# Two attention layers on one core: layer 1's regrouping transfers handed out one at a time, its next loads in 128 KB pieces, small transfers on GpSimd's queue

## The chip, the cores and the metric

The kernel runs on one core of a Trainium2 chip. Its time is the device time of one execution in microseconds (us). A core has a matrix engine (TensorE, PE in the profile, with its weight loads shown apart as PEld), VectorE (DVE), ScalarE (ACT), GpSimd (POOL) and SyncE (SP). SP computes nothing here: it issues DMA transfers, in the order in which they are written, and stops at a transfer whose semaphores have not come yet. All transfers run on the core's 16 DMA engines.

## The reference

```
x = x + layer0(groupnorm(x))     # 8 images, 512 channels, 32*32 = 1024 tokens
x = x + layer1(groupnorm(x))
```

Layer 0 is an attention with 8 heads after another group norm. Layer 1, which the change concerns, is an attention that mixes its heads before the softmax and normalises after it:

```
q, k, v = w_q x, w_k x, w_v x              # 8 heads of 64
attn = (q.k) * scale                       # per head, 1024 x 1024
attn = einsum('gh,bhqT->bgqT', w_head, attn)
attn = softmax(attn);  attn = (attn - mean) / sqrt(var + eps) * gamma + beta
out  = w_proj (attn . v) + b_proj
```

Everything is float32.

## The kernel before

**Stages.** Layer 0 runs first, image by image, and leaves its result in DRAM (`x1_d`). Layer 1 then takes the eight images in turn (`for b in range(B)`, from about 2000 us of the profile on). One image is an attention stage of 37 half-steps and a stage of projections (keys and values of the next image, output of this one, queries of the next one), in which TensorE is filled by large products.

**A half-step.** `Attention1.half_step(x, ag)` does six groups of products on TensorE, for several stages of the pipeline at once: `scores(x, 0)`, `mix(y, 0)`, `values(w, 0)`, `scores(x, 1)`, `mix(y, 1)`, `values(w, 1)`, with `y = x - 4` (`MLAG`) and `w = x - 5`. `x` counts 32 half-steps (`NX`) and then some that only drain the pipeline. `scores` makes q.k for two heads; VectorE or ScalarE copies the result into a tile `raw[t]`, `t = x // 2`. When `x` is odd the tile is complete: 128 partitions by 16 KB. To mix heads, heads must lie along the partitions, so the tile is rearranged by DMA: `regroup(t)` issues eight transfers of 256 KB (`R_ORDER`), each from every eighth partition of `raw[t]` to a tile `re[t, r]`. `mix` multiplies these by the small matrix `wmix` (32 products in the source for each of its two calls, 64x64 blocks; two of its calls use the same eight tiles), and ScalarE takes the exponential. In the next half-step `squares`, `sum_e`, `sum_e2` and `values` use it.

**Order.** The order of instructions on every engine is the order in which the code is written; an `Agenda` (`ag.at(x, f)`) puts a function at the end of a given half-step. Buffers set the rest: `raw` has two buffers, so the first copy of tile t+2, in half-step 2t+4, must wait until all eight transfers of tile t have landed; `re` has sixteen, so the transfers of tile t reuse tiles that `mix` reads up to the second call of half-step 2t+1. Scores, mix, totals and projections share three PSUM buffers (`m_psum`).

**SP's queue before the change.** In an odd half-step the eight regrouping transfers are issued together, between `scores(x, 1)` and `mix(y, 1)` in the program's order. In the same queue, from the agenda, are: the next image's input (`load_y`, four transfers of 512 KB after half-steps 6, 8, 10, 12) and its key and value weights (`load_w`, 256 KB each, after half-steps 14 to 28), and, three times in an image before the last time, the small transfers of the softmax's sums. For the latter, `totals(qb)` sums by products and copies a row, and two transfers `c<-row` spread it over partitions; two half-steps later `reciprocals(qb)` takes 1/x and writes it to DRAM (`zd<-rz`), and two transfers read it back to all partitions (`rzb<-zd`, 256 KB each); `divide(qb)` multiplies with it, after half-step x+5.

Of the kernel before, what the change touches and what calls it, by code (L numbers as in the profile page):

```python
# [9 lines left out]
F32 = mybir.dt.float32  # L10
# [8 lines left out]
P = 128  # L19
# [448 lines left out]
def tile_two_attention_layers(  # L468
# [527 lines left out]
    with ExitStack() as l1:  # L996
# [27 lines left out]

        y_t, qo_t, k_t, v_t, w_t = {}, {}, {}, {}, {}

        def load_w(key, src, chunks=range(NCC)):
            tag = {"v": "wtB", "p": "wp"}.get(key[0], "wtA")
            for c in chunks:
                if c == 0:  # L1030
                    w_t[key] = wtpool.tile(
                        [P, NCC, C], F32, tag=tag, name=f"w{key[0]}_{key[1]}"
                    )
                nc.sync.dma_start(out=w_t[key][:, c], in_=src[ts(c, P)])
# [230 lines left out]
        class Attention1:  # L1265
            def __init__(self, b):
                self.b = b
                self.raw, self.re, self.e, self.e2 = {}, {}, {}, {}

            def scores(self, x, i):  # L1270

                b, t, hp = self.b, x // 2, x % 2 * 2 + i
                qb, kb = t // NKB, t % NKB
                nm = f"s1_{b}_{x}_{i}"
                ps = m_psum(nm)
                pv = ps.rearrange("p m (j k) -> p m j k", j=2)
                for j in range(2):
                    for c in range(2):
                        for m in range(2):
                            r = slice(m * D, m * D + D)  # L1280
                            nc.tensor.matmul(  # L1281
                                pv[c * D : c * D + D, m, j],
                                qo_t[b][r, 2 * qb + j, hp, ts(c, D)],
                                k_t[b][r, hp, ts(kb, KB)], start=True, stop=True,
                            )
                if x % 2 == 0 and i == 0:
                    self.raw[t] = rawpool.tile([P, H, 2, KB], F32, tag="raw", name=f"raw_{b}_{t}")
                dst = self.raw[t][:, 2 * hp : 2 * hp + 2]
                if i == 0 and (x < MLAG or x % 2):
                    nc.vector.tensor_copy(dst, pv)  # L1290
                else:
                    nc.scalar.copy(dst, pv)  # L1292

            def regroup(self, t):

                raw = self.raw.pop(t)
                for r in R_ORDER:
# [3 lines left out]
                    nc.sync.dma_start(out=self.re[t, r], in_=raw[r::NR])  # L1301

            def mix(self, y, j):

                t, kc = y // 2, y % 2
                if j == 0:
                    self.e[y] = epool.tile([P, 2, T], F32, tag="e", name=f"e1_{self.b}_{y}")
                ps = m_psum(f"m1_{self.b}_{y}_{j}")
                for r in R_ORDER:
                    for c in range(2):  # L1310
                        k0 = kc * P + c * D
                        for a in range(2):
                            rows = slice(a * D, a * D + D)
                            nc.tensor.matmul(  # L1314
                                ps[c * D : c * D + D, a, ts(r, D)],
                                self.re[t, r][rows, j, k0 : k0 + D],
                                wmix[rows].rearrange("p g i -> p (g i)"),
                                start=True, stop=True,
                            )
                nc.scalar.activation(self.e[y][:, j], ps.rearrange("p a c -> p (a c)"), AF.Exp)  # L1320

            def squares(self, y, j):
                if y % QLAG == 0:
# [23 lines left out]
            def values(self, y, w):  # L1347

                b, t, kc = self.b, y // 2, y % 2
                kc = t % NKB * 2 + kc  # L1350
                if kc == 0 and w == 0:
                    self.acc = [
                        ps_a.tile([P, 2, QB], F32, tag=f"a{i}", name=f"a1_{b}_{y}_{i}")
                        for i in range(2)
                    ]
                e = self.by_head(self.e[y].rearrange("p j c -> p (j c)"))
                for g in range(4 * w, 4 * w + 4):
                    s, two = g // 2 % 2, g % 2
                    nc.tensor.matmul(  # L1359
                        self.acc[w][two * D : two * D + D, s].rearrange(  # L1360
                            "p (c i) -> p c i", i=Q8
                        ),
                        v_t[b][:, kc, ts(g, D)], e[:, g],
                        start=(kc == 0 and s == 0), stop=(kc == NT - 1),
                        skip_group_check=True,
                    )

            def leave(self, qb):

# [12 lines left out]
            def totals(self, qb):  # L1382


                ps = m_psum(f"t_{self.b}_{qb}")
                row = e2pool.tile([P, 2, FB], F32, tag="e2", name=f"row_{self.b}_{qb}")
                for m, z in ((1, self.z2), (0, self.z)):
                    for c in range(4):
                        nc.tensor.matmul(  # L1389
                            ps[c * 32 : c * 32 + 32, m].rearrange(  # L1390
                                "p (g c i) -> p g c i", g=4, i=Q8
                            ),
                            ones[:, :32],
                            self.by_head(z[:, c // 2])[:, c % 2 * 4 : c % 2 * 4 + 4],
                            start=True, stop=True, tile_position=(0, c * 32),
                        )
                nc.vector.tensor_copy(row[:, 1], ps[:, 1])
                nc.scalar.copy(row[:, 0], ps[:, 0])
                self.rows = []
                for m in range(2):  # L1400
                    c = stat.tile([P, 16], F32, tag=f"c{m}", name=f"c{m}_{self.b}_{qb}")
                    nc.sync.dma_start(out=c, in_=row[0::32, m])
                    self.rows.append(c)

            def reciprocals(self, qb):

                b = self.b
                zc, z2c = self.rows
                rz = stat.tile([P, 16], F32, tag="rz", name=f"rz1_{b}_{qb}")
                nc.vector.reciprocal(rz, zc)  # L1410
                zd = dram.tile([2, T], F32, tag=f"zd_{b}_{qb}", name=f"zd_{b}_{qb}")
                nc.sync.dma_start(out=zd, in_=rz)
                self.rzb = zpool.tile([P, T], F32, tag="rzb", name=f"rzb_{b}_{qb}")
                for two in range(2):
                    nc.sync.dma_start(
                        out=self.rzb[two * D : two * D + D], in_=zd[two].partition_broadcast(D)
                    )
# [55 lines left out]
            def half_step(self, x, ag):  # L1473
# [21 lines left out]
                    self.values(w, 0)  # L1495
                if x < NX:
                    self.scores(x, 1)
                    if x % 2:
                        self.regroup(x // 2)
                if 0 <= y < NX:  # L1500
                    self.mix(y, 1)
                if 0 <= w < NX:
                    self.values(w, 1)
                    self.e.pop(w)
                    if w % QLAG == QLAG - 1:
                        qb = w // QLAG
                        self.totals(qb)
                        if qb < NQB - 1:
                            ag.at(x + 2, lambda: self.reciprocals(qb))
                            ag.at(x + 5, lambda: self.divide(qb))  # L1510
                ag.run(x)


# [16 lines left out]
        for b in range(B):  # L1530
# [107 lines left out]
```

## Time and profile before

| what | value |
|---|---|
| median of 11 runs | 4574.57 us (4559.16 to 4720.16) |
| the profiled execution's own time | 4585.32 us |
| its span, first to last instruction | 4583.4 us |
| TensorE clock granted, mean | 0.995 |
| PE busy | 4383.5 us (96%) |
| DVE, ACT busy | 2475.5 us (54%), 2286.5 us (50%) |
| attention stage of one image, 2330 to 2512 us: PE, DVE, ACT busy | 167.76, 140.32, 147.65 of 182 us |
| the same stage: DMA share, bytes | 0.73 of 16 engines, 185 GB/s |
| regrouping transfers | 1024 of 256 KB, all from SP |

A line of a group of instructions reads: source line, engine, operation, what it writes and reads, shapes, how often; then busy time and the mean of one in ns; then the idle time of the engine just before them and what ended most of it. "issue" is idle time that ended with nothing that the profile can name. A wait is put down to the latest of the events that it waited for. The DMA share is the mean busy share of the 16 DMA engines.

### The profile page before, as it was taken

The page shows a single profiled execution, that of the slowest core. Times are in us where ns is not written, and L with a number is a line of the kernel's source. Part 1 is how long each engine was busy: PE and PEld are TensorE (multiplying, and loading weights), DVE is VectorE, ACT ScalarE, POOL GpSimd, SP SyncE. Part 2 cuts the span into 40 slices and gives each one's busy share as a digit, 9 for nine tenths or more (in the row PEclk, how much of TensorE's full clock was granted, in tenths as well). Part 3 has the DMA queues.
Part 4 walks back from the last instruction along what each step waited for, and adds up shares of the span by engine and source line. Part 5 has one row for each costly group of instructions (what it writes and reads, how often), then busy time and mean ns, then how long its engine had stood idle before and what let it go on. Part 6 is the DMA issues. An engine that isn't in the chain of part 4 may idle for free.

```text
span 4583.4 us, 129918 instructions
## 1 busy us (share of the span) xinstructions
PE 4383.5 (96%) x58560; PEld 2243.0 (49%) x58560; DVE 2475.5 (54%) x3396; ACT 2286.5 (50%) x2651; POOL 6.6 (0%) x14
## 2 busy tenths in 40 slices
PE   7999999999999999899999999999999999999998
PEld 3343434343434343356466466465466465465565
DVE  1727272727272727258367367376277276376376
ACT  1707070707070706058267277177177276276385
POOL 0000000000000000000000000000000000000000
PEclk9999999999999999999999999999999999999999
DMA  2010101010101000257267176275275375374464
GB/s 74 16 42 16 42 16 42 16 42 16 42 16 42 16 23 16 79 147 185 69 165 186 53 187 162 70 187 146 75 193 134 94 177 131 107 180 115 115 164 128
DMA packets 242885, 426.38 MB, mean 93 GB/s; under 512 B 63120, under 2 KB 63120, under 8 KB 242320
## 3 DMA queue, kind: packets, MB, share of 16 engines
q1 hardware_dynamic: 239744, 413.77, 33.7%
q8 instruction: 460, 7.54, 0.7%
q10 hardware_dynamic: 2304, 4.20, 0.3%
q14 instruction: 105, 0.86, 0.1%
q0 software_dynamic: 272, 0.02, 0.0%
HBM read 114.32 MB, written 34.08 MB: 32 GB/s over the span
## 4 chain that ended last, share of the span: by engine, by line
PE 92%; issue 3%; ACT 2%; DVE 2%; DMA 1%; SPq 1%; POOL 0%; DVEq 0%; POOLq 0%
PE a L1359 11%; PE s L1281 10%; PE m L1314 10%; PE a L876 9%; PE s L850 9%; PE pk L1081 5%; PE pk L797 5%; PE pv L1105 5%; PE pq L1137 5%; PE pq L797 5%; PE pv L820 5%; PE pp L797 5%; PE pp L1167 4%; PE t L1389 2%; PE z L898 1%
## 5 line engine op out<-in xcount | busy, mean ns | idle before, releaser
L1314 PE MATMUL m<-wmix,re 64*64 64x64 f32 x32768 | 612.1, 219 | 92.8 <-issue 86.0
L1314 PEld LDWEIGHTS m<-wmix,re 64*64 64x64 f32 x32768 | 593.5, 135 | 196.9 <-issue 134.0
L1320 ACT ACTIVATE e<-m 128x1024 f32<-128x1024 f32 x512 | 528.0, 1031 | 145.0 <-PE m L1314 141.7
L1359 PE MATMUL a<-e,v 128*64 128x256 f32 x4096 | 564.9, 393 | 33.2 <-ACT q L1380 20.9
L1337 DVE TENSOR_TENSOR z<-z,e 128x1024 f32<-128x1024 f32 x448 | 540.2, 1220 | 88.8 <-ACT e L1320 88.3
L1341 DVE TENSOR_TENSOR z<-z,e 128x1024 f32<-128x1024 f32 x448 | 535.6, 1220 | 75.4 <-ACT e L1330 75.0
L855 ACT ACTIVATE e<-s 128x1024 f32<-128x1024 f32 x512 | 498.4, 1026 | 147.9 <-PE s L850 147.9
L1281 PE MATMUL s<-k,q 64*64 64x256 f32 x8192 | 557.2, 389 | 6.0 <-issue 5.7
L850 PE MATMUL s<-q,k 64*64 64x512 f32 x4096 | 489.7, 591 | 3.0 <-ACT q L785 1.5
L863 DVE TENSOR_TENSOR zacc<-zacc,e 128x1024 f32<-128x1024 f32 x384 | 469.6, 1223 | 41.8 <-ACT e L855 15.3
L876 PE MATMUL a<-e,v 64*64 64x512 f32 x4096 | 484.1, 589 | 0.0
L1330 ACT ACTIVATE e<-e 128x1024 f32<-128x1024 f32 x448 | 461.7, 1061 | 0.0
L1292 ACT COPY raw<-s 128x1024 f32<-128x1024 f32 x368 | 373.1, 1016 | 165.7 <-PE s L1281 137.5
L1281 PEld LDWEIGHTS s<-k,q 64*64 64x64 f32 x8192 | 271.3, 133 | 270.7 <-issue 178.0
L1359 PEld LDWEIGHTS a<-e,v 128*64 128x64 f32 x4096 | 252.4, 136 | 156.8 <-issue 24.6
L876 PEld LDWEIGHTS a<-e,v 64*64 64x64 f32 x4096 | 156.6, 133 | 282.8 <-issue 282.8
L850 PEld LDWEIGHTS s<-q,k 64*64 64x64 f32 x4096 | 152.1, 133 | 286.8 <-issue 261.3
L1290 DVE COPY raw<-s 128x1024 f32<-128x1024 f32 x144 | 176.3, 1224 | 137.3 <-PE s L1281 116.2
L1081 PE MATMUL pk<-y,wk 128*128 128x512 f32 x512 | 230.3, 604 | 5.2 <-DVE y L1066 4.9
L797 PE MATMUL pp<-xa,wp 128*128 128x512 f32 x512 | 224.1, 598 | 5.9 <-DVE xa L938 5.9
L797 PE MATMUL pk<-n,w 128*128 128x512 f32 x512 | 225.5, 599 | 4.2 <-issue 4.2
L1105 PE MATMUL pv<-wv,y 128*128 128x512 f32 x512 | 225.5, 596 | 0.0
(190 smaller groups left out, 3276.0 us busy)
## 6 DMA issues: line engine op xcount, KB each, us to landing
re<-raw SPq DMA_DIRECT2D x1024, 256.0 KB
x<-in_x_dram SPq DMA_DIRECT2D x32, 512.0 KB
rzb<-zd SPq DMA_DIRECT2D x128, 128.0 KB
x<-x SPq DMA_DIRECT2D x32, 512.0 KB
y<-x SPq DMA_DIRECT2D x32, 512.0 KB
rzb<-zd SPq DMA_DIRECT2D x64, 256.0 KB
xs<-x SPq DMA_DIRECT2D x28, 512.0 KB
out_dram<-xs SPq DMA_DIRECT2D x28, 512.0 KB
```

The costliest lines, as they stand in the source:

```text
L797: nc.tensor.matmul(ps[:, f], w[:, c, o0 + oc * P : o0 + (oc + 1) * P], rhs[:, c, ts(f, FB)], start=(c == 0), stop=(c == NCC - 1),)
L850: nc.tensor.matmul(ps[c * D : c * D + D, m], k[r, hp, k0 : k0 + D], q[r, hp, ts(f, FB)], start=True, stop=True,)
L855: nc.scalar.activation(e[i], ps, AF.Exp)
L863: nc.vector.tensor_add(zacc[g], zacc[g], e[i])
L876: nc.tensor.matmul(acc[g][a][m * D : m * D + D], v[rows, kc, ts(2 * hp + m, D)], e[i][rows, m], start=(kc == 0), stop=(kc == NG - 1),)
L1281: nc.tensor.matmul(pv[c * D : c * D + D, m, j], qo_t[b][r, 2 * qb + j, hp, ts(c, D)], k_t[b][r, hp, ts(kb, KB)], start=True, stop=True,)
L1314: nc.tensor.matmul(ps[c * D : c * D + D, a, ts(r, D)], self.re[t, r][rows, j, k0 : k0 + D], wmix[rows].rearrange("p g i -> p (g i)"), star ...
L1320: nc.scalar.activation(self.e[y][:, j], ps.rearrange("p a c -> p (a c)"), AF.Exp)
L1330: nc.scalar.activation(e2, self.e[y][:, j], AF.Square)
L1337: nc.vector.tensor_add(self.z[:, j], self.z[:, j], self.e[y][:, j])
L1341: nc.vector.tensor_add(self.z2[:, j], self.z2[:, j], self.e2[j])
L1359: nc.tensor.matmul(self.acc[w][two * D : two * D + D, s].rearrange("p (c i) -> p c i", i=Q8), v_t[b][:, kc, ts(g, D)], e[:, g], start=(kc ...
```

## The change

In words:

- `regroup` no longer issues eight transfers together. After `scores(x, 1)` of an odd half-step (x of 5 to 31) the eight are put on a list (`self.due`), and one is taken from it after each of `mix(y, 0)`, `values(w, 0)`, `mix(y, 1)`, `values(w, 1)`. `behind(dma, ins)` adds a dependency: the transfer waits on SP until the last product of that group is done. Up to half-step 4, and from 32 on, what is on the list is issued at once, without this dependency.
- The next image's input and its key and value weights become pieces of 128 KB (`y_piece`: 32 partitions by 4 KB, 16 pieces; `w_piece`: 64 partitions by 2 KB, 8 pieces for each weight), on a list `self.pieces`; from half-step 5 on one is issued behind each `scores`. Before, they were 512 KB and 256 KB transfers from the agenda.
- `c<-row` and `zd<-rz` go to GpSimd's queue for the first three of an image's four blocks (`queue(qb)`). The two transfers `rzb<-zd` of these blocks are put at the head of the list of pieces one half-step after `reciprocals`. `divide` comes one half-step later.

The diff, cut to its core:

```diff
+        def behind(dma, ins):
+            tc.add_manual_dep(
+                dma.ins, ins.ins.name,
+                mybir.DependencyInfo(
+                    mybir.DependencyClass.Sync, mybir.DependencyReason.DATA
+                ),
+                reason="one at a time",
+            )
+        def w_piece(key, src, i):
...
+            c, r = i // 2, i % 2 * D
+            return nc.sync.dma_start(
+                out=w_t[key][r : r + D, c], in_=src[c * P + r : c * P + r + D]
+            )
+        def y_piece(b, i):
...
+            c, r = i // 4, i % 4 * 32
+            return nc.sync.dma_start(
+                out=y_t[b][r : r + 32, c], in_=x1_d[b][c * P + r : c * P + r + 32, :]
+            )
...
             def scores(self, x, i):
...
+                if x > MLAG:
+                    self.piece(last)
+                if x % 2 and i == 1:
+                    self.due = [(t, r) for r in R_ORDER]
...
-            def regroup(self, t):
-                raw = self.raw.pop(t)
-                for r in R_ORDER:
+            def regroup(self, ins=None, n=1):
+                for t, r in self.due[:n]:
                     self.re[t, r] = repool.tile(
                         [P, 2, KB], F32, tag="re", name=f"re_{self.b}_{t}_{r}"
                     )
-                    nc.sync.dma_start(out=self.re[t, r], in_=raw[r::NR])
+                    dma = nc.sync.dma_start(out=self.re[t, r], in_=self.raw[t][r::NR])
+                    if ins is not None:
+                        behind(dma, ins)
+                self.due = self.due[n:]
+            def piece(self, ins=None, n=1):
+                for fn in self.pieces[:n]:
+                    dma = fn()
+                    if ins is not None:
+                        behind(dma, ins)
+                self.pieces = self.pieces[n:]
...
             def mix(self, y, j):
...
+                self.regroup(last)
...
             def values(self, y, w):
...
+                self.regroup(last)
...
-                    nc.sync.dma_start(out=c, in_=row[0::32, m])
+                    self.queue(qb).dma_start(out=c, in_=row[0::32, m])
...
+            def queue(self, qb):
+                return nc.sync if qb == NQB - 1 else nc.gpsimd
-            def reciprocals(self, qb):
+            def reciprocals(self, qb, ag=None, x=None):
...
-                nc.sync.dma_start(out=zd, in_=rz)
+                self.queue(qb).dma_start(out=zd, in_=rz)
...
+                    ag.at(x + 1, lambda: self.pieces.__setitem__(slice(0, 0), spread))
...
                     self.scores(x, 1)
-                    if x % 2:
-                        self.regroup(x // 2)
                 if 0 <= y < NX:
                     self.mix(y, 1)
+                if x <= MLAG or x >= NX:
+                    self.regroup(n=NR)
+                if x >= NX:
+                    self.piece(n=len(self.pieces))
...
-                            ag.at(x + 2, lambda: self.reciprocals(qb))
-                            ag.at(x + 5, lambda: self.divide(qb))
+                            ag.at(x + 2, lambda: self.reciprocals(qb, ag, x + 2))
+                            ag.at(x + 6, lambda: self.divide(qb))
...
+                a.pieces += [lambda i=i: y_piece(b + 1, i) for i in range(4 * NCC)]
+                a.pieces += [lambda i=i: w_piece(("k", b + 1), wkT, i) for i in range(2 * NCC)]
+                a.pieces += [lambda i=i: w_piece(("v", b + 1), wvT, i) for i in range(2 * NCC)]
                 for c in range(NCC):
-                    ag.at(6 + 2 * c, lambda c=c: load_y(b + 1, [c]))
-                    ag.at(14 + 2 * c, lambda c=c: load_w(("k", b + 1), wkT, [c]))
-                    ag.at(22 + 2 * c, lambda c=c: load_w(("v", b + 1), wvT, [c]))
                     ag.at(24 + c, lambda c=c: normalize1(b + 1, [c]))
```

More of the change, by code (lines that the diff above doesn't have):

```diff
@@ L1025, in tile_two_attention_layers @@
         y_t, qo_t, k_t, v_t, w_t = {}, {}, {}, {}, {}
+        def behind(dma, ins):
+            tc.add_manual_dep(
+                dma.ins,
+                ins.ins.name,
+                mybir.DependencyInfo(
[4 more added lines that the diff above has]
+        def w_piece(key, src, i):
+            tag = {"v": "wtB", "p": "wp"}.get(key[0], "wtA")
+            if i == 0:
+                w_t[key] = wtpool.tile([P, NCC, C], F32, tag=tag, name=f"w{key[0]}_{key[1]}")
+            c, r = i // 2, i % 2 * D
[3 more added lines that the diff above has]
+        def y_piece(b, i):
+            if i == 0:
+                y_t[b] = ypool.tile([P, NCC, T], F32, tag="y", name=f"y_{b}")
+            c, r = i // 4, i % 4 * 32
+            return nc.sync.dma_start(
+                out=y_t[b][r : r + 32, c], in_=x1_d[b][c * P + r : c * P + r + 32, :]
+            )
         def load_w(key, src, chunks=range(NCC)):
@@ L1268, in __init__ @@
                 self.raw, self.re, self.e, self.e2 = {}, {}, {}, {}
+                self.due, self.pieces = [], []
             def scores(self, x, i):
@@ L1280, in scores @@
                             r = slice(m * D, m * D + D)
-                            nc.tensor.matmul(
+                            last = nc.tensor.matmul(
                                 pv[c * D : c * D + D, m, j],
@@ L1313, in mix @@
                             rows = slice(a * D, a * D + D)
-                            nc.tensor.matmul(
+                            last = nc.tensor.matmul(
                                 ps[c * D : c * D + D, a, ts(r, D)],
@@ L1358, in values @@
                     s, two = g // 2 % 2, g % 2
-                    nc.tensor.matmul(
+                    last = nc.tensor.matmul(
                         self.acc[w][two * D : two * D + D, s].rearrange(
@@ L1411, in reciprocals @@
                 zd = dram.tile([2, T], F32, tag=f"zd_{b}_{qb}", name=f"zd_{b}_{qb}")
-                nc.sync.dma_start(out=zd, in_=rz)
+                self.queue(qb).dma_start(out=zd, in_=rz)
                 self.rzb = zpool.tile([P, T], F32, tag="rzb", name=f"rzb_{b}_{qb}")
-                for two in range(2):
-                    nc.sync.dma_start(
-                        out=self.rzb[two * D : two * D + D], in_=zd[two].partition_broadcast(D)
-                    )
+                rzb = self.rzb
+                spread = [
+                    lambda two=two: nc.sync.dma_start(
+                        out=rzb[two * D : two * D + D], in_=zd[two].partition_broadcast(D)
+                    )
+                    for two in range(2)
+                ]
+                if ag is None:
+                    for fn in spread:
+                        fn()
+                else:
+                    ag.at(x + 1, lambda: self.pieces.__setitem__(slice(0, 0), spread))
                 col = B * H + NQB * b + qb
```

## The prediction

> **What bounds the kernel now.** I read the page first: PE is busy 4383.5 of 4583.4 us, and the chain that ended last is 92% PE and 3% "issue". So only TensorE's own pauses can be won, and I looked next at the groups of layer 1 and at who PE waited for from 2050 us on (columns: total us, times, longest).
>
> ```profile
> PE m L1314 <- issue: 80.5, 90, 2.7
> PE a L1359 <- ACT q L1380: 20.9, 24, 0.9
> PE a L1359 <- issue: 10.5, 14, 1.7
> PE t L1389 <- DVE z L1341: 6.1, 8, 0.9
> PE s L1281 <- issue: 5.3, 9, 1.2
> PE m L1314 <- DMA re<-raw: 4.6, 10, 0.9
> ```
>
> The reader should see that the data are hardly ever late (4.6 us for the regrouped tiles) and that 80.5 + 10.5 + 5.3 = 96 us end with nothing named. What is that? A pause in the middle of one `mix`, on the timeline of PE:
>
> ```profile
> 2748.08 0.75 PE L1314 MATMUL m<-wmix,re 64*64 64x64 f32 x39
> 2749.88 0.62 PE L1314 MATMUL m<-wmix,re 64*64 64x64 f32 x25 [1.04 <-issue]
> ```
>
> Its tiles had been used by the `mix` before it, so no transfer was missing. The DMA table has a kind of traffic that no line of the kernel issues:
>
> ```profile
> q1 hardware_dynamic: 239744, 413.77, 33.7%
> q8 instruction: 460, 7.54, 0.7%
> ```
>
> That is 460 packets of 16 KB: instructions. TensorE's two rows have 2 x 58,560 of them, 255 per packet. Laying the trace's packet records of q8 over PE's instructions, I find that 122 of layer 1's 159 PE pauses over 0.15 us (131.7 us in all) end between 1 and 2 us after the end of such a packet, and that most neighbouring pauses lie whole multiples of 256 instructions apart. These are late instruction fetches. What makes them late: of the fetches that began after 2.5 us in which the DMA engines were under 0.2 busy, 94 were followed by 0.013 us of pause in the mean; of those after more than 0.8 busy, 217 were followed by 0.44 us. SP's queue and the DMA share show where the full stretches come from:
>
> ```profile
> 2716.56 6.87 SPq L1301 DMA_DIRECT2D re<-raw  x8
> 2723.48 0.65 SPq L1034 DMA_DIRECT2D wk<-in_wkT_dram  x1
> 2730.87 6.60 SPq L1301 DMA_DIRECT2D re<-raw  x8
> ...
> 2716.50:2728.00 11.50, 11.14 (x338) 7.98 (x336) 9.99 (x16) 10.39 (x12) 0.00 (x0) 1.00 0.85 208
> 2753.90:2757.20 3.30, 3.10 (x88) 2.04 (x86) 3.30 (x4) 1.69 (x3) 0.00 (x0) 1.00 0.12 34
> ```
>
> The last two are stretches of time (PE, PEld, DVE, ACT, POOL busy, clock, DMA share, GB/s): a burst of eight, with one weight load, keeps the DMA engines 0.85 x 11.5 = 9.8 us busy; then they idle. So 256 KB costs 9.8/9 = 1.07 us of all engines; SP issues one in about 0.67 us (median), so two or three pile up.
>
> **What the Trainium skill says.** "Runtime: NRT & Kernel Launch", section "Instruction fetch mechanics": instructions come in blocks of 16 KiB (256 instructions) through a DMA queue of the sequencer's own, and the cost is "mostly hidden". The trace agrees on the block (7.54 MB / 460) and not on the hiding (96 us). "DMA: Bandwidth & Descriptors", "Queues, rings and completion order": a DMA engine alternates between queues by packet of some 9 to 17 descriptors, so a fetch waits at least for what is in service. A 256 KB transfer is eight 2 KB packets of the trace per engine, 1.07 us. On GpSimd's queue the same page ("Anatomy of one DMA") has about 2 us per transfer; this trace's eight small ones took 7.2 to 8.4 us, and I use those. "SBUF — State Buffer", "SBUF: two separate sides": GpSimd's descriptors can be held up by VectorE's fast copies; no run here shows it, and the copies in question take 0.69 us.
>
> **The change part by part.** Without pauses half of a half-step takes 2.97 us (scores start at 2716.59, 2719.56, 2722.53).
>
> 1. *Regrouping one by one.* Removed: the pile. Each 2.97 us two transfers are released, 2.14 us of DMA, plus a piece of 128 KB (half of 1.07: 0.53; a 512 KB input load shows 2.0 us): 2.67 us, a share of 0.90 where pieces run (38 in the 54 slots) and 0.72 elsewhere. The engines remain that full, but what a fetch finds ahead of it is one transfer, at most 1.07 us, rather than two or three. About 290 fetches fall in the attention stages; 96 us is 0.33 us each. Bounds: 0.013 us each (all relieved, saves 92 us) to 0.33 us (nothing). I take 0.125, about a quarter of the way from 0.013 to 0.44, since the share stays high and only the queue's depth falls: 36 us stay, **-60 us**.
>
> 2. *The last of the eight goes later.* Before, all eight were out about 7 us after the first; now the eighth waits for `values(w, 0)` of half-step 2t+3. From there to the copy that reuses `raw` lie scores 0.92 + mix 1.04 + values 1.01 + scores 0.92 = 3.89 us, and its products begin 0.91 us later (7/8 of a mix). An issue moves its first data 1.1 us after it starts (2712.43 to 2713.54 in the packet records); + 1.07 + some 0.3 to be seen (estimate) = 2.5 us. A piece ahead of it is served before (0.53 against 2.05 us of lead). Margin 1.4 us to the copy, 2.3 us to the products: 0 us. This is the step with least cover. If landing took 5 us or more, ScalarE, which has the copy in even half-steps and is busy 147.65 of 182 us, would stop 1.1 us for each of 112 tiles (14 of 16 per image x 8); its slack takes most of that.
>
> 3. *New waits on SP.* Each transfer waits for a product. Behind it in SP are only transfers whose products come later, in PE's own order; six issues per half-step at 0.55 to 0.67 us are 3.3 to 4.0 of 5.94 us: 0. The first of eight also waits for ScalarE's copy, as before (2716.54 end of copy, 2716.56 issue).
>
> 4. *Small transfers on GpSimd.* SP stood 433 us at `c<-row` (32 times, most of it at an image's end, which stays) and 107.6 us at `rzb<-zd`. Taking it away frees SP for about 3 us, 24 times; PE hardly waited on that, so 0 to -4 us. On GpSimd `c<-row` takes some 8 us after 2711.2, about 2720; `reciprocals` came at about 2723.9, at the faster pace 2723: hidden, margin 2 to 3 us; if late, VectorE stops, at most 2 us x 24, inside its slack (140.32 of 182). `zd<-rz` then lands near 2731.5, but the pieces `rzb<-zd` want issuing at the `scores` of x+4, near 2728.5: SP stops up to 3 us, as it did before (4.5 us at 2725). It delays the third and fourth of eight, which have over 5 us in hand: 0. `divide` one half-step later: nothing needs it before the output projection.
>
> 5. *Pieces.* Same bytes, 32 + 6 transfers where there were 12 + 6. They are done by half-step 24, when `normalize1` begins (32 pieces at two per half-step from 5 on end at 20, 6 spreads added): 0. Short packets relieve fetches as in 1.
>
> 6. *A faster PE meets ACT.* ACT's share in this stage rises from 81% to some 85%; more waits on exponentials: **+4 us** (0 to 12, from the 20.9 + 6.1 us of waits that exist).
>
> Unchanged: layer 0, projections, the start of an image (bursts up to half-step 4). Sum: -60 + 4 = -56 us against the profiled execution's 4585.3 (span 4583.4 and 1.9 around it) = 4529. That execution was 10.7 us above the median of the runs; against 4574.6 the same sum gives **4518 us**.
>
> **Rivals.** (a) *The DMA share decides, not the pile.* With 0.9 of the time busy a fetch finds a transfer nearly always, and what it wins from the depth is small. For it: the share, and the relation above is one of share. Against: lone 512 KB loads, with 2 us packets, count in the busy class, and shorter queues must shorten a wait in the worst case. Then 0 to 20 us are won: 4566. (b) *The eighth transfer becomes the bound*, and the kernel is slower. Place: SP's eighth issue, `raw`'s copy and `mix` in half-step 2t+4. It decides from 5.3 us of landing on: 0.5 us past the products' 4.8 us, times 112 tiles, is 56 us and eats the gain; at 6.3 us it is 170 - 56 = +112: 4690. For it: bursts of eight landed the last one some 11 us after the first issue, and ACT and DVE already waited 20 + 21 us on `re<-raw`. Against: that is queueing, which the change takes away, and nine of the thirteen such waits over 1 us lie in an image's first 40 us, before the single transfers are in force. (c) *The dependencies do nothing*, as SP runs behind PE anyhow: excluded, since SP issued eight in 6.9 us and then stood idle.
>
> **How the numbers follow.** The forecast has 0.68 (own range 4482 to 4550), (a) 0.17, half of it within 0.2% (9 us, about what can be told from no change), (b) 0.15, of which 0.01 within 0.2%. So faster 0.68 + 0.08 = 0.76, same 0.10, slower 0.14. Range 4482 (all fetches relieved) to 4572 (the most of rival (a)).
>
> **What would show it.** Right: PE's "issue" before L1314 falls from 86 to some 32 us; SP's timeline has single regrouping transfers; DMA share per microsecond stays above 0.7 without the empty stretches; "DMA re<-raw" under PE's waits stays below 10 us. Wrong: "issue" stays at 80 (a); ACT raw or PE m waiting on `re<-raw` for over 50 us (b); VectorE waiting for `c<-row` over 20 us (step 4).

## The result and the profile after

The changed kernel takes 4494.87 us (median of 8 runs, 4490.4 to 4502.06) against 4574.57 (median of 31 runs by then): a ratio of 0.9828, with a 95% interval of 0.9814 to 0.9842. The ratio leaves out one slow run of the kernel before, that of 4720.16 us. The change is 79.7 us, where 56 had been forecast; the range, 4482 to 4572, holds it. The profiled execution took 4497.62 us, its span 4495.8.

Who TensorE waited for in the changed kernel, from 2050 us on, the same view as of the kernel before (us in total, times, longest):

```profile
PE m L1360 <- issue: 30.2, 36, 2.4
PE a L1406 <- ACT q L1428: 20.0, 23, 0.9
PE m L1360 <- DMA re<-raw: 10.0, 18, 1.3
PE t L1437 <- DVE z L1388: 5.8, 8, 0.7
...
PE a L1406 <- issue: 3.1, 3, 1.5
...
PE s L1312 <- issue: 1.5, 2, 0.8
```

The three "issue" lines were 80.5 + 10.5 + 5.3 = 96.3 us and are 34.8; the wait for regrouped tiles has doubled, from 4.6 to 10.0 us; the rest stands nearly still. All 114 "issue" pauses of TensorE before, and all 41 after, end between 1 and 2 us after the end of an instruction packet, by the trace's packet records. At each of them TensorE has run 256 instructions for each packet that has landed, plus the same 192 or so (within 4): it goes on when the next block of 256 is there. The instruction packets are the same 460:

```profile
q1 hardware_dynamic: 232192, 413.18, 34.5%
q8 instruction: 460, 7.54, 0.7%
```

SP's queue on the timeline shows how the same bytes are now handed out:

```profile
2646.70 1.52 SPq L1336 DMA_DIRECT2D re<-raw  x2
2648.74 0.31 SPq L1053 DMA_DIRECT2D y<-x  x1
2649.67 1.85 SPq L1336 DMA_DIRECT2D re<-raw  x2
2651.71 0.45 SPq L1053 DMA_DIRECT2D y<-x  x1
```

A stretch around these rows, and the next, as sums (length, then PE, PEld, DVE, ACT, POOL busy, clock, DMA share, GB/s):

```profile
2646.00:2658.00 12.00, 12.00 (x365) 8.61 (x361) 11.12 (x11) 11.15 (x13) 0.00 (x0) 1.00 0.81 215
2658.00:2670.00 12.00, 10.96 (x311) 7.58 (x310) 9.17 (x8) 9.09 (x10) 0.00 (x0) 1.00 0.81 203
```

Two transfers and a piece every 3 us, in place of eight and then nothing. In thirty steps of 3 us (from 2700 us on before, from 2646 us on after) the share is under 0.5 in 10 before and in 2 after, and over 0.95 in 16 and in 7. So the DMA engines are not less busy, and TensorE runs 12 us in the first stretch without a pause.

Where the time came from, by the totals of the two profiled executions: the span fell by 4583.4 - 4495.8 = 87.6 us. PE's idle time fell from 199.9 to 136.9 us (63.0), and PE's busy time from 4383.5 to 4358.9 (24.6), with the same 58,560 products. The second part had not been foreseen. The kernel before shows what most of it is made of. Here is an undisturbed `mix`, to be laid beside the one at 2748.08 us that the prediction shows, which a late fetch cuts in two.

```profile
2745.11 1.11 PE L1314 MATMUL m<-wmix,re 64*64 64x64 f32 x64
```

The 64 products take 1.11 us in one go and 0.75 + 0.62 = 1.37 us in two. From the start of the mix to the start of the next group it is 1.04 us in one go and 2.34 us in two. So this pause costs 1.04 us that is listed and 0.26 us that is booked as busy; why, the profile does not show. Over 87 mixes that fetches cut (from 2050 us on, at the full clock) the second part is 0.30 us in the mean. Some 76 fewer pauses (118 before, 42 after, in layer 1) at 0.26 to 0.30 us are 20 to 23 of the 24.6 us (an estimate). A little more comes from the granted clock, which falls after some long pauses. One of 2.46 us for a fetch, and the stretch behind it, in the kernel before:

```profile
2421.21 1.24 PE L1314 MATMUL m<-wmix,re 64*64 64x64 f32 x35 [2.46 <-issue]
...
2421.00:2425.00 4.00, 3.79 (x55) 2.29 (x59) 3.21 (x3) 1.02 (x1) 0.00 (x0) 0.57 0.04 14
```

By the records of the clock, layer 1 before the change had five stretches of 3.4 us at half of it, four of them right after fetch pauses of 1.84 to 2.71 us; in the changed kernel such stretches sum to 10.2 instead of 17 us (the end of the program left out).

### The profile page after: what moved, and what is told of

It is laid out like the page before. It is cut to its first block, busy times and chain, and to the rows that moved or that the text cites. A ratio compares the mean times of both kernels' runs of the same rounds, so it can differ in the third digit from the quotient of the medians.

```text
span 4495.8 us, 130314 instructions
## 1 busy us (share of the span) xinstructions
PE 4358.9 (97%) x58560; PEld 2234.0 (50%) x58560; DVE 2471.8 (55%) x3396; ACT 2276.5 (51%) x2651; POOL 53.4 (1%) x86
## 4 chain that ended last, share of the span: by engine, by line
PE 91%; DMA 3%; ACT 2%; DVE 2%; issue 1%; SPq 1%; POOL 0%; DVEq 0%; POOLq 0%
PE a L1406 11%; PE s L1312 10%; PE m L1360 10%; PE a L876 10%; PE s L850 9%; PE pk L1111 5%; PE pk L797 5%; PE pv L1135 5%; PE pq L1167 5%; PE pq L797 5%; PE pv L820 5%; PE pp L797 5%; PE pp L1197 4%; DMA re<-raw 2%; PE t L1437 2%; PE z L898 1%
## 5 line engine op out<-in xcount | busy, mean ns | idle before, releaser
L1360 PE MATMUL m<-wmix,re 64*64 64x64 f32 x32768 | 599.1, 219 | 44.1 <-issue 31.1
L1406 PE MATMUL a<-e,v 128*64 128x256 f32 x4096 | 559.1, 393 | 24.1 <-ACT q L1428 20.9
L1325 DVE COPY raw<-s 128x1024 f32<-128x1024 f32 x144 | 176.2, 1224 | 90.9 <-PE s L1312 79.7
```

Source lines behind the costliest of these rows:

```text
L1360: last = nc.tensor.matmul(ps[c * D : c * D + D, a, ts(r, D)], self.re[t, r][rows, j, k0 : k0 + D], wmix[rows].rearrange("p g i -> p (g i)" ...
L1406: last = nc.tensor.matmul(self.acc[w][two * D : two * D + D, s].rearrange("p (c i) -> p c i", i=Q8), v_t[b][:, kc, ts(g, D)], e[:, g], sta ...
```

## Experiments

The theory: a fetch of TensorE's instructions waits behind the transfers that stand in the DMA queue when it is asked for, so their number counts, not the share of busy DMA engines. The rivals: large loads or SP's stops at small transfers were what cost; or the pauses come from the rate of fetching alone. "Issue pauses" below are the sum of PE's three "issue" waits in layer 1 from 1990 us on, in which measure the kernel before has 101.9 us and the changed one 35.7; waits for regrouped tiles are taken from 1990 us on too (6.0 and 11.9 us). Some expectations are for the pauses before the mix alone (85.7 and 31.1 us).

### 1. Regrouping one by one, alone

```diff
-                return nc.sync if qb == NQB - 1 else nc.gpsimd
+                return nc.sync
...
-                    ag.at(x + 1, lambda: self.pieces.__setitem__(slice(0, 0), spread))
+                for fn in spread:
+                    fn()
...
-                            ag.at(x + 6, lambda: self.divide(qb))
+                            ag.at(x + 5, lambda: self.divide(qb))
...
-                a.pieces += [lambda i=i: y_piece(b + 1, i) for i in range(4 * NCC)]
-                a.pieces += [lambda i=i: w_piece(("k", b + 1), wkT, i) for i in range(2 * NCC)]
-                a.pieces += [lambda i=i: w_piece(("v", b + 1), wvT, i) for i in range(2 * NCC)]
+                    ag.at(6 + 2 * c, lambda c=c: load_y(b + 1, [c]))
+                    ag.at(14 + 2 * c, lambda c=c: load_w(("k", b + 1), wkT, [c]))
+                    ag.at(22 + 2 * c, lambda c=c: load_w(("v", b + 1), wvT, [c]))
```

> The changed kernel with one part kept: regrouping transfers one behind each group of products. Loads of 512 and 256 KB from the agenda, small transfers and the reciprocals' spread on SP, division after half-step x+5, all as before the change. Theory (a fetch waits for the transfers queued ahead of it; the pile of eight is the pile that counts): most of the gain is here, 4500 to 4525 us, PE's issue pauses before the mix 35 to 50 us. Rival (the large loads or SP's stops at the small transfers were what cost): under a third of the gain, 4550 us or more, issue pauses above 65 us.

Measured: 4648.75 us, ratio 1.018 (1.0155 to 1.0206), slower than before the change. The time is where the rival had it (4550 us or more), but not for the rival's reason, which needed issue pauses above 65 us; the theory missed the time. PE's waits in this kernel:

```profile
PE m L1360 <- DMA re<-raw: 121.0, 78, 5.2
PE a L1406 <- ACT q L1428: 21.1, 24, 0.9
PE m L1360 <- issue: 16.4, 27, 1.4
```

Most fetch pauses are gone: 16.4 us before the mix, where 35 to 50 had been forecast, and 19.7 us in all. In their place TensorE waits for regrouped tiles. Where, the timeline of PE and SP shows, cut to the rows that matter and in order of time:

```profile
2399.44 0.60 SPq L1464 DMA_DIRECT2D zd<-rz  x1
...
2402.26 1.12 SPq L1468 DMA_DIRECT2D rzb<-zd  x2
...
2403.48 6.78 SPq L1336 DMA_DIRECT2D re<-raw  x5
...
2404.43 0.88 PE L1360 MATMUL m<-wmix,re 64*64 64x64 f32 x48
2408.11 0.49 PE L1360 MATMUL m<-wmix,re 64*64 64x64 f32 x8 [2.80 <-DMA re<-raw]
```

SP has issued `zd<-rz` and then stands, up to 2402.26, for it to land, since the next in its queue reads it back. The seventh and eighth regrouping transfers are behind that, and behind two transfers of 256 KB; the mix has done 48 of 64 products when it runs out of tiles. SP stands there three times in an image. The clock column of the same stretch shows a second price:

```profile
2400.00:2404.00 4.00, 4.00 (x103) 2.63 (x102) 4.00 (x4) 3.32 (x5) 0.00 (x0) 1.00 0.43 113
2404.00:2408.00 4.00, 1.31 (x60) 1.04 (x52) 2.77 (x3) 0.61 (x1) 0.00 (x0) 0.94 1.05 258
2408.00:2412.00 4.00, 3.32 (x32) 1.70 (x36) 0.73 (x1) 2.73 (x3) 0.00 (x0) 0.50 0.79 184
2412.00:2416.00 4.00, 4.00 (x92) 2.86 (x88) 1.63 (x2) 2.25 (x4) 0.00 (x0) 0.71 0.34 80
2416.00:2420.00 4.00, 4.00 (x128) 2.90 (x124) 3.04 (x3) 2.94 (x4) 0.00 (x0) 1.00 0.89 238
```

After the pause TensorE's granted clock is 0.50 for 4 us and 0.71 for the next 4. Over the whole run the mean clock is 0.981 instead of 0.995; 0.014 of 4643 us is 65 us (an estimate), a large part of what this kernel loses to the changed one.

### 2. Eight together again, the rest of the change kept

```diff
                     self.scores(x, 1)
+                    self.regroup(n=NR)
...
-                if x <= MLAG or x >= NX:
-                    self.regroup(n=NR)
...
             def mix(self, y, j):
...
-                self.regroup(last)
...
             def values(self, y, w):
...
-                self.regroup(last)
```

> The changed kernel with the eight regrouping transfers issued together again, where they were before, without the dependency on products; pieces and GpSimd's queue kept. Theory: most of the gain is lost, 4545 to 4575 us, issue pauses before the mix 65 to 90 us. Rival (loads or SP's stops): 4530 us or less.

Measured: 4560.26 us, ratio 0.9981 (0.9971 to 0.9991), issue pauses 91.4 us, of them 78.7 before the mix. As the theory said: pieces, GpSimd's queue and the later spread are worth some 9 us without the single transfers. So neither part of the change does it without the other, and the gains don't add: single transfers alone lose 80 us, the rest alone wins 9, together they win 80.

### 3. Small transfers on SP

```diff
-                return nc.sync if qb == NQB - 1 else nc.gpsimd
+                return nc.sync
```

> The changed kernel with the small transfers of the sums on SP's queue for all blocks. Theory: SP stops a few us three times in an image, single transfers catch up, 4493 to 4507 us. Rival (SP's stops are dear, since the last of eight has little in hand): 4515 us or more, with PE and ACT waiting for regrouping transfers 30 us more than in the changed kernel.

Measured: 4493.88 us (0.9839, 0.9813 to 0.9865), issue pauses 30.0 us, waits for regrouped tiles 11.3 us. GpSimd's queue gives nothing that can be measured.

### 4. Two groups of four

```diff
             def mix(self, y, j):
...
-                self.regroup(last)
+                if j:
+                    self.regroup(last, 4)
...
             def values(self, y, w):
...
-                self.regroup(last)
```

> The changed kernel with the eight transfers in two groups of four, each behind the second mix of a half-step. Bytes and DMA share are the same; four queue up where one did: by issues of 0.67 us and service of 1.07 us some 2.3 us stand in the queue at most (estimate), against 3.4 us for eight. Theory (depth of the queue): between the two, 4525 to 4555 us, issue pauses 50 to 75 us. Rival (only the share of busy DMA engines counts, the depth doesn't, and the gain is from elsewhere): 4490 to 4505 us, as the changed kernel.

Measured: 4542.22 us (0.9938, 0.9922 to 0.9955), issue pauses 64.3 + 7.6 + 3.7 = 75.6 us. Between the two, as the depth of the queue had it. The DMA share (the figure before the last) does not tell this kernel, first, from the changed one:

```profile
2320.00:2490.00 170.00, 156.63 (x4403) 108.33 (x4407) 129.21 (x137) 138.03 (x153) 5.26 (x8) 1.00 0.76 188
2320.00:2490.00 170.00, 163.76 (x4661) 113.53 (x4664) 137.06 (x151) 145.66 (x162) 5.83 (x9) 1.00 0.79 195
```

### 5. One behind each group of products

```diff
                 if x > MLAG:
                     self.piece(last)
+                    self.regroup(last)
```

> The changed kernel with a regrouping transfer behind each group of scores too, so that the eight are out after eight groups of products instead of eleven or so, and then a gap. Bytes are the same. One is released each 0.99 us and takes 1.07 us, with pieces between, so at the end of the eight about two stand in the queue (estimate). Theory (depth): some of the fetch pauses come back, issue pauses before the mix 35 to 60 us, waits for regrouped tiles fall under 6 us, 4500 to 4525 us. Rival (room before the eighth transfer is what is short in the changed kernel): 4490 us or less.

Measured: 4533.93 us (0.9901, 0.9874 to 0.9929), issue pauses 56.6 + 7.0 + 4.2 = 67.8 us, waits for regrouped tiles 4.7 us. The transfers are still released one by one, but faster than they are served. Theory right in kind; the time was 9 us above its upper end. More room for the eighth took away 7 us of waits for tiles and brought 32 us of fetch pauses: room for it is not what the changed kernel is most short of.

### 6. Each transfer two places later

```diff
-                    self.due = [(t, r) for r in R_ORDER]
+                    if x == MLAG + 1:
+                        self.due += [None, None]
+                    self.due += [(t, r) for r in R_ORDER]
...
```

> The changed kernel with each regrouping transfer two groups of products later, so the eighth goes behind the second values of half-step 2t+3. By the prediction's sum 0.92 us are then left to the copy and 1.83 us to the products of the eighth, against 2.5 us of landing: ScalarE stops 1.6 us and TensorE 0.7 us for each of 112 tiles. Theory (the eighth has little in hand, and this is the cliff that the first experiment fell over): waits of PE for regrouped tiles 60 us or more, 4550 to 4640 us. Rival (the first experiment was slow for another reason, and the eighth has room): 4510 us or less.

Measured: 4754.56 us (1.0391, 1.0363 to 1.0419).

```profile
PE m L1362 <- DMA re<-raw: 203.0, 227, 3.0
PE a L1408 <- ACT q L1430: 20.9, 24, 0.9
PE m L1362 <- issue: 8.2, 7, 2.1
```

The cliff is where the theory put it, and higher: 203 us instead of 0.7 x 112 = 78, beside 180.6 us of ScalarE's own wait with `raw`. 203 us over 112 tiles is 1.8 us per tile; the sum behind the prediction left the eighth's products 1.83 us, so its landing would take some 1.83 + 1.8 = 3.6 us, not 2.5 (an estimate which counts all waits against the eighth, where 91 us are for the seventh). The trace gives it directly: from the start of SP's issue to the product that waited for it, the eighth took 3.9 us (median of 106 such waits). With that, in the changed kernel nothing is left of the 3.9 us to the copy, and 0.9 us of the 4.8 to the products. The 15 eighths that TensorE waits for there took 5.5 us (median), so the late ones take longer still. That ScalarE's wait came out at the forecast 1.6 x 112 = 179 us is chance: it is 68 waits of 2.7 us. The mean clock is 0.985.

### 7. The kernel before with half of the transfers

```diff
-                for r in R_ORDER:
+                for r in R_ORDER[::2]:
...
-                                self.re[t, r][rows, j, k0 : k0 + D],
+                                self.re[t, r % 4][rows, j, k0 : k0 + D],
```

> The kernel before with four of the eight regrouping transfers left out: the products of the other four read the tiles of the first four, so the mixed scores are other values, with the same instructions on TensorE. Theory (fetches wait behind the transfers): issue pauses before the mix fall from 86 to 35 to 60 us, 4505 to 4540 us. Rival (fetches are late by their own rate, whatever the DMA engines do): issue pauses above 75 us, 4560 us or more.

Measured: 4470.49 us (0.9771, 0.9745 to 0.9797), with issue pauses of 25.7 us, 22.4 of them before the mix.

```profile
PE m L1314 <- issue: 22.4, 40, 1.1
PE a L1359 <- ACT q L1380: 21.0, 24, 0.9
PE t L1389 <- DVE z L1341: 7.2, 8, 1.9
PE a L1359 <- issue: 3.0, 5, 1.4
```

TensorE runs the same instructions at the old pace of fetching; only transfers are gone, and the pauses with them. The rate of fetching alone is excluded as the cause. The drop is larger than expected. It also gives a mark: 108 us below the kernel before, of which the change gets 80 with all transfers in place.

### 8. Experiment 1 with the spread moved

```diff
-                for fn in spread:
-                    fn()
+                    ag.at(x + 1, lambda: self.pieces.__setitem__(slice(0, 0), spread))
...
-                            ag.at(x + 5, lambda: self.divide(qb))
+                            ag.at(x + 6, lambda: self.divide(qb))
```

> The first experiment (one transfer behind each group of products, large loads from the agenda, small transfers on SP) with one thing more of the change: the reciprocals' two spread transfers go behind scores one half-step later, and the division with them. Theory (in the first experiment SP stood at the spread, waiting for the write to DRAM, just ahead of the seventh and eighth transfer, 24 times, and the clock fell after such pauses): waits of PE for regrouped tiles fall from 121 to under 35 us, the mean clock is back above 0.99, 4500 to 4530 us. Rival (the large loads were what made the eighth late): 4600 us or more.

Measured: 4514.09 us (0.9859, 0.9831 to 0.9887), mean clock 0.997, waits for regrouped tiles 24.9 us, issue pauses 29.3 + 5.0 + 1.1 = 35.4 us. These two moved transfers, three times in an image, together with the later division, make 135 us of difference to experiment 1 (147 by the ratios). What is left to the changed kernel, 19 us (14 by the ratios), is put down to the large loads, since experiment 3 has GpSimd's queue at nothing: ScalarE waits 61.8 us with `raw` for regrouping transfers here, and 34.8 there.

### 9. The change with the spread at once

```diff
-                    ag.at(x + 1, lambda: self.pieces.__setitem__(slice(0, 0), spread))
+                for fn in spread:
+                    fn()
```

> The changed kernel with one thing undone: the reciprocals' two spread transfers follow the write to DRAM at once on SP's queue. Theory (SP stands there for the write's landing, just before the seventh and eighth regrouping transfer): the loss of the first experiment is here, 4590 to 4650 us, waits of PE for regrouped tiles over 80 us, mean clock below 0.99. With the write on GpSimd's queue it lands later than from SP, so it is not better than in the first experiment but for the loads. Rival (with pieces in place of large loads the queue catches up in time): 4530 us or less.

Measured: 4590.21 us (1.0035, 1.0025 to 1.0045), waits for regrouped tiles 82.2 us with a longest of 4.5, mean clock 0.987. Undoing this one edit takes away the whole gain of the change, and 16 us more.

### 10. Pieces spread thinner

```diff
-                if x > MLAG:
+                if x > 8 and (i == 0 or x >= 24):
                     self.piece(last)
```

> The changed kernel with the pieces spread thinner: none before half-step 9, one for each half-step until 24, then two. The share of busy DMA engines in the first two thirds of an image falls by some 0.09 (0.53 of 5.94 us). Theory: fewer fetches find something ahead of them, and the image's start has fewer waits for regrouped tiles: issue pauses 20 to 30 us, 4475 to 4492 us. Rival (what is left of the pauses doesn't depend on the pieces): 4492 to 4500 us.

Measured: 4489.18 us (0.9817, 0.98 to 0.9834), issue pauses 24.5 + 5.5 + 0.3 = 30.3 us, waits for regrouped tiles 6.8 us. Both waits fell as the theory had it, but the interval overlaps that of the changed kernel (0.9814 to 0.9842): 6 us better at the median, not shown to be better.

### 11. In addition, the first two together

```diff
             def regroup(self, ins=None, n=1):
+                if ins is not None and len(self.due) == NR:
+                    n = 2
```

> As the thinner pieces, and the first two of the eight regrouping transfers together behind the first mix (they leave SP almost together in the changed kernel as well, since the first waits for ScalarE's copy), so that each later one goes one group of products earlier. Theory: one place more in hand for the eighth takes most of the remaining waits of PE and ScalarE for regrouped tiles, at no new pile: 2 to 8 us faster than with the thinner pieces alone. Rival (the two make a pile for a fetch): same or slower than these by up to 10 us.

Measured: 4529.19 us (0.9904, 0.9885 to 0.9924), issue pauses 51.4 + 8.3 + 1.9 = 61.6 us. The move of six transfers by one group of products cost 40 us, four times the rival's worst. Waits for regrouped tiles did fall, to 5.6 us. SP's rows suggest why so small a move counts: the first transfer waits for ScalarE's copy as well, so first, second and third now left together. Counting the transfers on SP in layer 1 that were issued within 1.7 us of the second one before them, there are 353 in this kernel, 188 with thinner pieces alone and 148 in the changed kernel; 449 in experiment 5 and in the kernel before. The count is a rough guide: experiment 5 has far fewer pauses than the kernel before, at the same 449. The depth in the table below is a better one: over 512 KB stood in the queue for 0.18 of the time here, for 0.07 with thinner pieces alone.

### 12. No two together

```diff
-                if x > MLAG:
+                if x > MLAG + 1 and x % 2 == 0 and i == 0:
+                    self.regroup(last)
+                if x > 8 and (i == 1 or x >= 24):
                     self.piece(last)
...
-                    self.due = [(t, r) for r in R_ORDER]
+                    self.due = [None] + [(t, r) for r in R_ORDER]
...
```

> The changed kernel with thinner pieces (from half-step 9, one for each half-step until 24, behind the second scores) and the first two regrouping transfers drawn apart: the first behind the values of the odd half-step, the second behind the first scores of the next, the other six where they are in the changed kernel. The eighth is not moved. Theory (even two or three transfers that leave together make a pile for a fetch, as two drawn together cost some 40 us in the eleventh experiment): issue pauses under 25 us, 4470 to 4487 us. Rival (the eleventh was slow for another reason, such as a phase between fetches and transfers that happened to fit badly): no better than the thinner pieces, 4487 us or more.

Measured: 4488.35 us (0.9815, 0.9797 to 0.9833), issue pauses 34.6 + 5.2 + 0.5 = 40.3 us. The rival had the time right: drawing the first two apart gives nothing over the thinner pieces. But the transfers were not drawn apart: the count of threes is 224, more than with thinner pieces alone, and the depth rose from 0.07 to 0.11. By the code, a piece behind the second scores now stands near others. So the last step of the theory, that pairs cost too, is neither shown nor excluded.

### Together

All kernels with every regrouping transfer in place, and without a late eighth, in the order of their issue pauses. The depth is worked out from SP's rows and the packet records: the share of the attention stages (within 4 us of a product of `mix`) in which over 512 KB, two regrouping transfers, had been issued by SP and not yet moved.

| kernel | issue pauses, us | depth | waits for regrouped tiles, us | median, us |
|---|---|---|---|---|
| small transfers on SP (3) | 30.0 | 0.08 | 11.3 | 4493.9 |
| thinner pieces (10) | 30.3 | 0.07 | 6.8 | 4489.2 |
| spread moved, large loads (8) | 35.4 | 0.15 | 24.9 | 4514.1 |
| changed kernel | 35.7 | 0.08 | 11.9 | 4494.9 |
| no two together (12) | 40.3 | 0.11 | 5.6 | 4488.4 |
| first two together (11) | 61.6 | 0.18 | 5.6 | 4529.2 |
| one behind every group (5) | 67.8 | 0.24 | 4.7 | 4533.9 |
| groups of four (4) | 75.6 | 0.21 | 4.8 | 4542.2 |
| groups of eight (2) | 91.4 | 0.31 | 2.0 | 4560.3 |
| before | 101.9 | 0.36 | 6.0 | 4574.6 |

The depth goes with the pauses, though not in every step; with half of the transfers (7) it is 0.13, at 25.7 us.

The packet records also show the fetches starting late. TensorE has one block of 256 instructions in hand when it comes to the point, the same in every block, near which a fetch starts if the DMA engines are free; it stops if those 256 run out. Before the change, a fetch started 24 instructions behind that point (median) when the engines had been under 0.2 busy for 2.5 us, and 133 behind it when they had been over 0.8 busy. In the changed kernel these last start 85 behind it, at the same share. At 352 instructions in 5.94 us that is 1.8 us of delay before and 1.0 us after (estimates), as two or three transfers ahead of the fetch, or one, would give. The packet itself takes about as long in both (1.18 and 1.08 us, medians in layer 1). What is left open is whether a fetch also has to meet the transfers in a certain phase, the rival of experiment 12.

From before to the changed kernel 66.2 us of pauses went with 79.7 us of time, 1.20 us for one, close to the 0.26 us beside each 1.04 us. The two waits mostly pull against each other: what shortens the queue lets the last transfer go later.

## Why the prediction was right

**The main step, transfers one by one (-60 us).** It held: the pauses from 2050 us on fell by 61.5 us and left 34.8, where 36 was taken. That close a hit is in part luck: the 0.125 us for each fetch was a choice between two bounds, not worked out, and the 290 fetches are too few, since the packet records have 352 of them in the attention stages. Experiments 2, 4 and 5 show that it is the pile that counts, and experiment 7 that the transfers are the cause. Rival (a), that the share decides, is excluded by experiment 4 with a share of 0.76 against 0.79, and by the fetches themselves: those that began after 2.5 us in which the DMA engines were over 0.8 busy are 217 before and 222 after, but the pause behind them fell from 0.44 to 0.14 us in the mean. The step was priced too low: it took the idle time for the whole price of a pause. Between the two profiled executions the span fell by 87.6 us, 31.6 more than the 56; 24.6 of these are PE's busy time, and 7.0 idle time. The share itself came out lower than worked out: 0.81 instead of 0.90 where pieces run.

**The last of eight (0 us).** PE's waits for regrouped tiles rose by 5.9 us, and ScalarE's by some 15, while VectorE's fell from 21.1 to 8.0. The landing of 2.5 us was the term that was mis-sized: experiment 6 has 3.9. Part of it, the 0.3 us "to be seen", had nothing behind it. Rival (b) was right in place and kind, and so close that three delays of a few us in an image (experiments 1 and 9) turn the change into a loss. The prediction asked at which landing time this decides; it did not ask what in SP's queue could delay the eighth.

**Small transfers (0 to -4 us), with the third and fourth transfers delayed at no cost.** Right for what the change does, by experiment 3. But it was taken for a small convenience, when the spread's new place is what carries the main step: 135 us between experiments 1 and 8. In the changed kernel SP stands at `rzb<-zd` for 14.5 us, 8 times, all that is left of 107.6 us, 32 times; with GpSimd's `zd<-rz` landing after 3.5 us (median), not the 7 to 8 that were taken, the stop of up to 3 us did not come. "As it did before", said of SP's stop, was no argument: before, the eighth had gone long ago, and afterwards the same stop in the old place is 121 us of waits.

**Pieces (0 us).** Too low: 14 to 19 us between experiment 8 and the changed kernel, by fewer waits for `raw` and for tiles. The fetch pauses are alike there (35.4 and 35.7 us), so short packets did not relieve fetches, as the step suggested. Nor were the packets of the large loads long: a 512 KB load is 4 KB packets of 0.16 us (kernel before, 2713.5 to 2715.7 us); the 2 us of the prediction are the load's.

**ACT met by a faster PE (+4 us).** It didn't come: PE's waits for ScalarE stayed at 20.9 us (from 1990 us on). That about as much was lost to regrouped tiles makes the sum right there by chance.

**Dependencies on SP (0 us), rival (c).** SP does stop at them: 348.5 us for `mix` and 157.5 for `values` from 2050 us on, and what stands behind them is for later by the program's order. So they do something, and (c) is out.

## What to carry to other kernels

When the busiest engine pauses and the profile names nobody, look at whether the pauses lie a fixed number of instructions apart, and at what the DMA queue holds then: in this kernel instructions came through DMA as well, and transfers issued together went with late ones even where the data had time to spare. Spacing out transfers buys that back, but it spends the room of the last one; so take out of the queue, just ahead of it, everything that is large or at which the queue can stall. And count a pause at more than its idle time: some 1.2 us of time went with each us of it here.

## What was not expected of the hardware

- TensorE's granted clock dropped after long pauses, whether data or a fetch ended them: in experiment 1, after a wait of 2.80 us for data and some stop-and-go, to 0.50 for 4 us and 0.71 for the next 4; in the kernel before, after fetch pauses of 2.46 and 2.71 us, to 0.57 (2421 to 2425 us) and 0.68 (3676 to 3680 us). After a pause of 1.88 us (2727.8 to 2729.7 us) it stayed at 1.00, after one of 1.84 us (up to 3478.0 us) it was 0.68 for 4 us. So the length alone does not decide; what does was not tested.
- A transfer of 256 KB among others of its kind took 3.9 us from its issue to the product that waited for it (experiment 6), where adding its parts gave 2.5.
- Six transfers moved by one group of products, about 1 us each, cost 40 us (experiment 11 against 10).
